# A graph network's start, chunk norms and polynomial: block pattern in three transfers, unit 1 behind unit 0's products, last norm pass on VectorE, first polynomial term a stage ahead

## The chip, the cores and the metric

The kernel runs on one core of one Trainium2 chip. The metric is the device time of one execution in microseconds (us). The executions of one kernel spread over 3 to 10 us, so each kernel was timed several times beside the kernel before on the same chip. Every run of this study was in the fast state, so no state has to be sorted out. Engines: TensorE (PE; its weight loads are PEld), VectorE (DVE), ScalarE (ACT), GpSimd (POOL) and SyncE (SP, which here only issues transfers).

## The reference, cut to what matters

128 graphs of 64 nodes with 256 features pass four layers. Each is `x = layernorm(x + layer(x))`.

```python
# layer 0: five groups of nodes, two graph convolutions each, mixed by softmax(fusion_w)
for g, idx in enumerate(GROUPS):
    h     = relu(norm_adj(adj_g) @ (x_g @ W1[g]) + b1[g])       # 256 -> 512
    out_g = relu(norm_adj(adj_g) @ (h @ W2[g]) + b2[g])         # 512 -> 256
    fused[:, idx] += softmax(fusion_w)[g] * out_g
# layer 1: one symmetric-normalised convolution
# layer 2: polynomial  conv_w[0] + conv_w[1] An + conv_w[2] An^2 + conv_w[3] An^3, applied to x @ W.T, leaky relu
# layer 3: five gated recurrent steps;  m = h @ weight[l];  agg = (adj != 0).T @ m;  h = gru(agg, h)
```

## The kernel before

Layer 0 is done in 16 **units** (some graphs of one group packed into four tiles of up to 126 rows). Layers 1 to 3 work on 16 **chunks** of 8 graphs; the first two chunks' layers 1 and 2 run beside the last units, the rest beside the recurrent steps of earlier chunks. TensorE's order is the program's order. The order of the other engines is found by a scheduler when the kernel is built, from the data dependences and its own estimate of when each thing is ready. This turns out to be the point of the case.

```python
def norm_apply(y, mv, rs, nb, by="v", n=NP, r=128):      # last pass of a layer norm; "a": ACT, "v": DVE
    ...
        if by[p] == "a":
            nc.scalar.activation(v, v, AF.Identity, bias=nb[:r, p : p + 1], scale=rs[:r, p : p + 1])
        else:
            e.tensor_scalar(v, v, mv[:r, p, 0:1], rs[:r, p : p + 1], op0=ALU.subtract, op1=ALU.mult)

def mid(c):                                   # layers 1 and 2 of chunk c, in stages
    a64 = adjs.pop(c)
    Ab = ...; nc.vector.tensor_mul(Ab, a64, pair)          # first to need the chunk's adjacency
    ...                                                    # rsum, rinv, dinv1, dg, An on DVE
    yield
    ...
    nc.scalar.activation(poly, p, AF.Identity, scale=cw[:, 3:4])
    nc.vector.scalar_tensor_tensor(poly, dg, cw[:, 2:3], poly, op0=ALU.mult, op1=ALU.add)
    ...
    norm = norm_stats(xt, "a")                             # twice in a chunk
    yield
    norm_apply(xt, *norm, "a")

def prep(i):                                  # unit i: normalised adjacency A, its transpose AT
    ...
    nc.vector.tensor_add(ae, a, eye0)                      # needs the transfer of a
    ...                                                    # deg, dinv, A = ae * block0
    nc.tensor.transpose(p, A, ident)                       # pT
    evictions.append(nc.vector.tensor_mul(AT, p, dinv))

def aggregate(i): ...                         # pa = xg.T AT  -> ag (ACT copy)
def hidden(i): ...                            # ph = W1 ag    -> hg (ACT relu)
def support(i): ...                           # ps = hg W2    -> s  (ACT copy)
def add(i): ...                               # po = s AT     -> z  (ACT relu, scaled by the softmax)

def others(i): layernorm(XO[i])               # layer 0's norm of the nodes in no group: ten x blocks "xo"
... (cut: other definitions)

block0 = const(c_block0, [TR, 5, TR], "block0", nc.scalar, w0)
...
for i in range(-2, NU + 1):
    if i >= 0: stage(load0, i + 3)
    stage(add, i - 1)
    stage(aggregate, i + 1)
    stage(support, i)
    ...
    if i == -1:
        with tc.issue_after(evictions[0].ins): prep(1)
    else: stage(prep, i + 2)
    if i < 0:
        load0(i + 3, powers[-1]); load_weights(i + 4)
    stage(hidden, i + 1)
    for f, o in ((store_others, i - 1), (others, i), (load_others, i + 2)):
        if 0 <= o < 10: f(o)
    if i == -1: ...                           # softmax of fusion_w: fm, fe (ACT), fs, fr, gw
    elif i == 1: ...                          # late constants on GpSimd's queue; brz = bih + bhh
```

More names in the traces: pp is the product of An with poly (twice in a chunk), h is ACT's copy of the transposed state in a recurrent step, which the product pa of that step (L209) reads, and pf is a product of weights formed once between the two parts. Ab is the first tile of a chunk's polynomial.

Of the kernel before, what the change touches and what calls it, by code (L numbers as in the profile page):

```python
# [9 lines left out]
F32 = mybir.dt.float32  # L10
# [57 lines left out]
def gnn_stack(  # L68
# [58 lines left out]
    def norm_stats(y, by="v", n=NP, r=128):  # L127

        by = (by * n)[:n]
        st = small.tile([128, NP, 6], F32, name="st")  # L130
        mv = small.tile([128, NP, 2], F32, name="mv")
        for p in range(n):
            nc.vector.bn_stats(st[:r, p, :], y[:r, p, :])  # L133
            nc.vector.bn_aggr(mv[:r, p, :], st[:r, p, :])
        ve = small.tile([128, NP], F32, name="ve")
        nc.vector.tensor_scalar(ve[:r, :n], mv[:r, :n, 1], EPS_LN, None, op0=ALU.add)  # L136
        rs = small.tile([128, NP], F32, name="rs")
        nc.gpsimd.tensor_tensor(rs[:r, :n], ve[:r, :n], mhalf[:r, :n], ALU.pow)  # L138
        nb = None
        if "a" in by:  # L140
            nb = small.tile([128, NP], F32, name="nb")
            nc.vector.scalar_tensor_tensor(nb[:r, :n], mv[:r, :n, 0], -1.0, rs[:r, :n], op0=ALU.mult, op1=ALU.mult)  # L142
        return mv, rs, nb

    def norm_apply(y, mv, rs, nb, by="v", n=NP, r=128):
        by = (by * n)[:n]
        for p in range(n):
            v = y[:r, p, :]
# [3 lines that stand above are left out]
                e = nc.vector if by[p] == "v" else nc.gpsimd  # L152
                e.tensor_scalar(v, v, mv[:r, p, 0:1], rs[:r, p : p + 1], op0=ALU.subtract, op1=ALU.mult)
# [64 lines left out]
    def mid(c):  # L218

        a64 = adjs.pop(c)  # L220


        Ab = keep.tile([128, NP, 128], F32, name="Ab", bufs=1)
        nc.vector.tensor_mul(
            Ab.rearrange("p q (b m) -> p q b m", b=2),
            a64[:, :, None, :].to_broadcast([128, NP, 2, N]),
            pair[:, None, :, :].to_broadcast([128, NP, 2, N]),
        )
        A01 = keep.tile([128, NP, 128], F32, name="A01", bufs=4)
        nc.vector.tensor_scalar(A01, Ab, 0.0, None, op0=ALU.not_equal)  # L230
        rsum = small.tile([128, NP], F32, name="rsum")
        nc.vector.tensor_reduce(rsum, a64, AX.X, ALU.add)
        rdeg = small.tile([128, NP], F32, name="rdeg")
        nc.vector.tensor_scalar(rdeg, rsum, 1.0, None, op0=ALU.add)
        rinv = small.tile([128, NP], F32, name="rinv")
        nc.vector.tensor_scalar(rinv, rsum, 1e-9, None, op0=ALU.add)
        nc.vector.reciprocal(rinv, rinv)
        dinv1 = inv_sqrt(rdeg, NP, 128, "d1")

        nc.vector.tensor_scalar(rsum, rsum, 1e-9, None, op0=ALU.add)  # L240
        dg = keep.tile([128, NP, 128], F32, name="dg", bufs=1)
        nc.vector.tensor_mul(
            dg, ident[:, None, :].to_broadcast([128, NP, 128]), rsum[:, :, None].to_broadcast([128, NP, 128])
        )
        An = keep.tile([128, NP, 128], F32, name="An", bufs=1)
        nc.vector.tensor_mul(An, Ab, rinv[:, :, None].to_broadcast([128, NP, 128]))
        yield


        AT1 = keep.tile([128, NP, 128], F32, name="AT1", bufs=1)  # L250
        poly = keep.tile([128, NP, 128], F32, tag="poly", name="poly3", bufs=2)
        p = psum("pT1").rearrange("p (q n) -> p q n", q=NP)
        for q in range(NP):
            nc.tensor.transpose(p[:, q, :], Ab[:, q, :], ident)
        nc.scalar.activation(poly, p, AF.Identity, scale=cw[:, 3:4])

        nc.vector.scalar_tensor_tensor(poly, dg, cw[:, 2:3], poly, op0=ALU.mult, op1=ALU.add)

        nc.vector.tensor_add(AT1, p, ident[:, None, :].to_broadcast([128, NP, 128]))
        nc.vector.tensor_mul(AT1, AT1, dinv1[:, :, None].to_broadcast([128, NP, 128]))  # L260
        yield
        xt = xts.pop(c)
        p = psum("pp").rearrange("p (q n) -> p q n", q=NP)
        for q in range(NP):
            nc.tensor.matmul(p[:, q, :], An[:, q, :], poly[:, q, :], start=True, stop=True)
        poly = keep.tile([128, NP, 128], F32, tag="poly", name="poly1", bufs=2)
        nc.vector.scalar_tensor_tensor(poly, dg, cw[:, 1:2], p, op0=ALU.mult, op1=ALU.add)
        ag = gather(xt, AT1, "ag1")
        nc.vector.tensor_add(xt, xt, l1bs[:, None, :].to_broadcast([128, NP, D]))
        p = psum("pp").rearrange("p (q n) -> p q n", q=NP)  # L270
        for q in range(NP):
            nc.tensor.matmul(p[:, q, :], An[:, q, :], poly[:, q, :], start=True, stop=True)
        poly = keep.tile([128, NP, 128], F32, tag="poly", name="poly0", bufs=2)
        nc.vector.scalar_tensor_tensor(poly, dg, cw[:, 0:1], p, op0=ALU.mult, op1=ALU.add)
        yield
        for u in range(NP // 2):
            p = psum("pd").rearrange("p (q d) -> p q d", q=2)
            for h in range(2):
                q = 2 * u + h
                for k in range(2):  # L280
                    nc.tensor.matmul(  # L281
                        p[:, h, :], ag[:, k, q * 128 : (q + 1) * 128], L1W[:, k, :], start=k == 0, stop=k == 1
                    )
            for h in range(2):
                q = 2 * u + h
                nc.vector.scalar_tensor_tensor(
                    xt[:, q, :], p[:, h, :], dinv1[:, q : q + 1], xt[:, q, :], op0=ALU.mult, op1=ALU.add
                )
        norm = norm_stats(xt, "a")
        yield  # L290
        norm_apply(xt, *norm, "a")
        yield


        ag = gather(xt, poly, "ag2")
        yield
        for u in range(NP // 2):
            p = psum("pd").rearrange("p (q d) -> p q d", q=2)
            for h in range(2):
                q = 2 * u + h  # L300
                for k in range(2):
                    nc.tensor.matmul(  # L302
                        p[:, h, :], ag[:, k, q * 128 : (q + 1) * 128], L2W[:, k, :], start=k == 0, stop=k == 1
                    )
            v = keep.tile([128, 2, D], F32, name="v", bufs=1)
            for h in range(2):
                q = 2 * u + h
                nc.scalar.activation(v[:, h, :], p[:, h, :], AF.Identity, bias=cb, scale=rinv[:, q : q + 1])
            nc.vector.scalar_tensor_tensor(v, v, 0.2, v, op0=ALU.mult, op1=ALU.max)  # L309
            nc.vector.tensor_add(xt[:, 2 * u : 2 * u + 2, :], v, xt[:, 2 * u : 2 * u + 2, :])  # L310
        norm = norm_stats(xt, "a")
        yield
        norm_apply(xt, *norm, "a")
        state[c] = (xt, A01)
        yield

# [11 lines left out]
    with ExitStack() as c0:  # L328
# [187 lines left out]
        eye0 = const(c_eye0, [TR, 5, NJ], "eye0", nc.scalar, w0)  # L516
        load0(0)
        ident = const(c_ident, [128, 128], "ident", nc.scalar)
        block0 = const(c_block0, [TR, 5, TR], "block0", nc.scalar, w0)
        nc.vector.memset(F, 0.0)  # L520
        b1 = const(b1T, [128, NG * 4], "b1", nc.scalar, w0)
        b2c = const(b2.rearrange("g (k p) -> p (g k)", p=128), [128, NG * 2], "b2", nc.scalar, w0)
        fw = spread(fusion_w, NG, "fw", w0, nc.scalar)

        def load_weights(g):
            nc.sync.dma_start(W1[:, g], w1[g].rearrange("(k p) e -> p k e", p=128))
            nc.sync.dma_start(W2[:, g], w2[g].rearrange("(k p) e -> p k e", p=128))

        load_weights(1)

        def products(l, q):

# [22 lines left out]
        for i in range(-2, NU + 1):  # L555
            if i >= 0:
                stage(load0, i + 3)
            stage(add, i - 1)
            stage(aggregate, i + 1)
            early_stage(i, 0)  # L560
            stage(support, i)
            if i == NU:
                folds = [products(0, q) for q in range(3)]
            stage(finish, i - 1, g0)
            early_stage(i, 1)
            if i == -1:

                with tc.issue_after(evictions[0].ins):
                    prep(1)
            else:  # L570
                stage(prep, i + 2)
            if i < 0:
                load0(i + 3, powers[-1])
                load_weights(i + 4)
            stage(hidden, i + 1)
            early_stage(i, 2)
            if i == 0:
                for g in (4, 0):
                    load_weights(g)
            for f, o in ((store_others, i - 1), (others, i), (load_others, i + 2)):  # L580
                if 0 <= o < 10:
                    f(o)
            if i == -1:

                with tc.issue_after(evictions[0].ins):
# [366 lines left out]
```

## Time and profile before

| | before |
|---|---|
| time, median (3 runs; later 6 beside the changed kernel) | 2249.12 us (2248.47) |
| profiled span | 2248.5 us |
| TensorE busy / idle | 2187.8 / 60.7 us |
| ACT / VectorE busy | 1064.2 / 1369.1 us |
| first wait of pp, in the first chunk's polynomial (unit 12's pa is done by then) | 225.44 us |

TensorE is busy 97% of the span, so the reader should look only at who TensorE waits for, and where. The prediction below shows those waits and the places. One place deserves a second look, because its label misled: the 3.38 us at 22.04, which the list of waits puts down to fs. This is VectorE's timeline just before it (start, duration, engine, line, operation, what was written from what; in brackets the idle time before and what ended it):

```profile
20.33 0.43 DVE L133 BATCH_NORM_STATS2 st<-xo 128x6 f32<-128x256 f32 x1 [3.69 <-DMA xo<-in_x_dram]
20.67 0.14 DVE L124 SCALAR_TENSOR_TENSOR d0o<-deg,d0r 126x4 f32<-126x4 f32 x1
...
21.34 0.65 DVE L381 TENSOR_TENSOR A<-ae,block 126x504 f32<-126x504 f32 x1
```

VectorE sat 3.69 us in front of a norm of an x block that had not landed. Behind it in its order stood d0o and A of unit 1, which TensorE needed. A norm that nobody waited for held up the start.

### The profile page before, as it was taken

Reading aid. Unit: us, or ns where it says so; the run is one execution under the profiler, and the core shown is the slowest. Engines: PE = TensorE matmul, PEld = TensorE weight load, DVE = VectorE, ACT = ScalarE, POOL = GpSimd, SP = SyncE. Lnnn points to the kernel's source line nnn. Section 1 sums busy time; section 2 is a strip of 40 time slices with the busy share of each in tenths; the row PEclk is TensorE's granted clock in tenths of the full one; section 3 lists DMA queues with packets and bytes.
Section 4 is the critical chain, followed back from the end, with each engine's and each line's share of the span. In section 5 each row is a group of like instructions: output and inputs, shape, how many; then the busy total and the mean of one; then the engine's idle time right before and its main releaser. Section 6 shows DMA issues by size and latency. Waiting matters only on the chain.

```text
span 2248.5 us, 30146 instructions
## 1 busy us (share of the span) xinstructions
PE 2187.8 (97%) x11526; PEld 1909.7 (85%) x11526; DVE 1369.1 (61%) x2972; ACT 1064.2 (47%) x1978; POOL 603.4 (27%) x639
## 2 busy tenths in 40 slices
PE   6999999999999999999999999999999999999997
PEld 4677788888888888888888888888888888888886
DVE  4543656665766666665756675657665666556546
ACT  2333444445545455445454455455455544455443
POOL 3210123222223223223223232222222232232222
PEclk9999999999999999999999999999999999999998
DMA  6531110000100000000100010001000000000000
GB/s 199 162 118 34 46 43 3 1 3 1 41 1 3 1 20 22 3 1 10 31 1 3 1 40 1 3 1 41 1 1 1 19 10 1 1 10 10 1 1 19
DMA packets 53892, 51.12 MB, mean 23 GB/s; under 512 B 20598, under 2 KB 48630, under 8 KB 53748
## 3 DMA queue, kind: packets, MB, share of 16 engines
q1 hardware_dynamic: 49524, 43.90, 6.4%
q0 software_dynamic: 1936, 4.83, 0.7%
q8 instruction: 91, 1.49, 0.3%
q10 hardware_dynamic: 2288, 0.47, 0.1%
q14 instruction: 53, 0.43, 0.1%
HBM read 32.40 MB, written 16.78 MB: 22 GB/s over the span
## 4 chain that ended last, share of the span: by engine, by line
PE 75%; DVE 13%; ACT 3%; DMA 3%; SPq 2%; issue 2%; POOL 1%; ACTq 0%; POOLq 0%; DVEq 0%
PE parz L688 20%; PE pan L688 10%; PE pdrz L688 10%; PE pa L209 7%; PE pdn L688 5%; PE pbrz L688 5%; PE pT L729 3%; PE ps L430 3%; PE pbn L688 3%; PE pd L281 2%; PE ph L416 2%; DVE st L133 1%; PE pd L302 1%; DMA xo<-in_x_dram 1%; DVE v L309 1%
## 5 line engine op out<-in xcount | busy, mean ns | idle before, releaser
L705 ACT COPY c<-parz 128x512 f32<-128x512 f32 x240 | 140.6, 586 | 343.1 <-PE parz L688 343.0
L688 PE MATMUL parz<-Th,WHH 128*128 128x256 f32 x960 | 285.8, 379 | 0.0
L688 PE MATMUL parz<-Ta,V 128*128 128x256 f32 x960 | 285.6, 379 | 0.0
L668 POOL TENSOR_TENSOR Th<-hn 128x512 f32<-128x512 f32 x64 | 89.3, 1395 | 651.5 <-DVE hn L789 642.1
L786 ACT ACTIVATE NI<-NI,bih 128x512 f32<-128x512 f32 x160 | 115.1, 719 | 191.6 <-DVE NI L782 191.4
L688 PEld LDWEIGHTS parz<-Ta,V 128*128 128x128 f32 x960 | 182.4, 190 | 24.8
L668 POOL TENSOR_TENSOR Ta<-agg 128x512 f32<-128x512 f32 x80 | 101.6, 1270 | 377.9 <-ACT agg L212 377.9
L705 ACT COPY c<-pan 128x512 f32<-128x512 f32 x240 | 140.8, 587 | 127.4 <-PE pan L688 127.4
L688 PEld LDWEIGHTS parz<-Th,WHH 128*128 128x128 f32 x960 | 176.2, 190 | 20.8 <-ACT c L705 0.2
L717 DVE TENSOR_TENSOR RZ<-pdrz,c 128x512 f32<-128x512 f32 x80 | 55.1, 689 | 200.7 <-PE pdrz L688 200.6
L759 ACT ACTIVATE RZ<-RZ,brz 128x512 f32<-128x512 f32 x160 | 106.7, 715 | 117.0 <-DVE RZ L717 117.0
L688 PE MATMUL pan<-Ta,V 128*128 128x256 f32 x480 | 143.1, 380 | 0.9 <-ACT c L705 0.9
L688 PE MATMUL pan<-Th,WHH 128*128 128x256 f32 x480 | 142.8, 379 | 0.0
L711 DVE TENSOR_TENSOR NI<-pbn,c 128x512 f32<-128x512 f32 x80 | 55.3, 691 | 137.5 <-PE pbn L688 135.1
L209 PEld LDWEIGHTS pa<-A,h 128*128 128x128 f32 x1024 | 123.2, 192 | 17.8 <-ACT h L803 15.2
L209 PE MATMUL pa<-A,h 128*128 128x128 f32 x1024 | 126.1, 276 | 9.6 <-ACT h L803 9.6
L138 POOL TENSOR_TENSOR rs<-ve,mhalf 128x4 f32<-128x4 f32 (+2 forms) x66 | 67.7, 1026 | 248.3 <-DVE ve L136 248.3
L707 DVE TENSOR_TENSOR NI<-pdn,c 128x512 f32<-128x512 f32 x80 | 55.2, 690 | 118.8 <-ACT c L705 118.8
L150 ACT ACTIVATE xt<-xt,nb,rs 128x256 f32<-128x256 f32 x186 | 99.6, 595 | 52.0 <-DVE nb L142 51.8
L787 DVE TENSOR_TENSOR RZ<-hn,NI 128x512 f32<-128x512 f32 x128 | 87.9, 687 | 53.0 <-ACT NI L786 53.0
L789 DVE TENSOR_TENSOR hn<-RZ,NI 128x512 f32<-128x512 f32 x160 | 109.6, 685 | 1.8
L788 DVE TENSOR_TENSOR RZ<-RZ 128x512 f32<-128x512 f32 x160 | 109.5, 684 | 1.8
(199 smaller groups left out, 5147.1 us busy)
## 6 DMA issues: line engine op xcount, KB each, us to landing
out_dram<-xt SPq DMA_DIRECT2D x32, 256.0 KB
W<-in_w_dram SPq DMA_DIRECT2D x10, 512.0 KB
xt<-xb SPq DMA_DIRECT2D x32, 156.0 KB
xo<-in_x_dram SPq DMA_DIRECT2D x9, 512.0 KB
xb<-xo SPq DMA_DIRECT2D x9, 512.0 KB
xt<-xa SPq DMA_DIRECT2D x32, 100.0 KB
xg<-in_x_dram SPq DMA_DIRECT2D x25, 125.0 KB
xa<-xg SPq DMA_DIRECT2D x25, 125.0 KB
```

The source lines that it names most:

```text
L138: nc.gpsimd.tensor_tensor(rs[:r, :n], ve[:r, :n], mhalf[:r, :n], ALU.pow)
L150: nc.scalar.activation(v, v, AF.Identity, bias=nb[:r, p : p + 1], scale=rs[:r, p : p + 1])
L209: nc.tensor.matmul(p[:, q * 128 : (q + 1) * 128], src[:, q, k * 128 : (k + 1) * 128], m[:, q, :], start=True, stop=True)
L430: nc.tensor.matmul(p[: u.rows[t], t - v, :], hg[:, e, u.off[t] : u.off[t] + u.rows[t]], W2[:, u.g, e, :], start=e == 0, stop=e == 3,)
L668: nc.gpsimd.tensor_sub(t[:, 0:2, :], a[:, :, H:], a[:, 0, :].rearrange("p (s n) -> p s n", s=2))
L688: nc.tensor.matmul(bank[:, g, :], w[:, q, i - 1, :], rhs, start=i in (1, 2, 5) and g == 0 and m == 0, stop=m == len(side) - 1, skip_group_ ...
L705: nc.scalar.copy(c, self.a)
L759: nc.scalar.activation(RZ[:, q, 0, :], RZ[:, q, 0, :], AF.Sigmoid, bias=b[0])
L786: nc.scalar.activation(n, n, AF.Tanh, bias=bih[:, 4 + j : 5 + j])
L787: nc.vector.tensor_sub(d, self.hT[:, j, :], n)
L788: nc.vector.tensor_mul(d, d, z)
L789: nc.vector.tensor_add(self.hn[:, j, :], d, n)
```

## The change

The intent: let TensorE begin sooner (only the block's first part must land; unit 0's products no longer stand behind unit 1's transposes; the weights' loads are split so that data come in the order of need), take the chunk norms' last pass off ACT, where they stood ahead of copies that TensorE waits for, and form the polynomial's second-degree term while the transposes still run. The ten x norms move one unit later.

```diff
@@ mid
+        poly = keep.tile([128, NP, 128], F32, tag="poly", name="poly3", bufs=2)
+        nc.scalar.activation(poly, dg, AF.Identity, scale=cw[:, 2:3])
         An = keep.tile([128, NP, 128], F32, name="An", bufs=1)
 ... (cut: next stage)
-        nc.scalar.activation(poly, p, AF.Identity, scale=cw[:, 3:4])
-        nc.vector.scalar_tensor_tensor(poly, dg, cw[:, 2:3], poly, op0=ALU.mult, op1=ALU.add)
+        nc.vector.scalar_tensor_tensor(poly, p, cw[:, 3:4], poly, op0=ALU.mult, op1=ALU.add)
 ... (cut; the next four lines twice)
-        norm = norm_stats(xt, "a")
+        norm = norm_stats(xt)
         yield
-        norm_apply(xt, *norm, "a")
+        norm_apply(xt, *norm)
@@ start
-        block0 = const(c_block0, [TR, 5, TR], "block0", nc.scalar, w0)
+        block0 = w0.tile([TR, 5, TR], F32, name="block0")
+        for ks in (slice(1, 2), slice(2, 5), slice(0, 1)):
+            nc.scalar.dma_start(block0[:, ks], c_block0[:, ks])
 ... (cut: load_weights becomes load_first for W1 and load_second for W2)
-            stage(aggregate, i + 1)
+            if i:
+                stage(aggregate, i + 1)
             stage(support, i)
+            if not i:
+                aggregate(1)
             if i == -1:
+                hidden(0)
                 with tc.issue_after(evictions[0].ins):
                     prep(1)
             else:
                 stage(prep, i + 2)
-            if i < 0:
-                load0(i + 3, powers[-1])
-                load_weights(i + 4)
-            stage(hidden, i + 1)
+                stage(hidden, i + 1)
+            if i == -2:
+                load0(1, powers[0]); load_second(1); load0(2, powers[0]); load_first(2)
+            elif i == -1:
+                load_second(2); load_first(3)
+            elif i == 0:
+                load_second(3)                      # then both of groups 4 and 0
 ... (cut: the old place of the loads of groups 4 and 0)
-            for f, o in ((store_others, i - 1), (others, i), (load_others, i + 2)):
-                if 0 <= o < 10:
-                    f(o)
+            for f, j in ((store_others, i - 1), (others, i), (load_others, i + 2)):
+                for o in range(10):
+                    if min(o + 1, 9) == j:
+                        f(o)
```

More of the change, by code (lines that the diff above doesn't have):

```diff
@@ L250, in mid @@
         AT1 = keep.tile([128, NP, 128], F32, name="AT1", bufs=1)
-        poly = keep.tile([128, NP, 128], F32, tag="poly", name="poly3", bufs=2)
         p = psum("pT1").rearrange("p (q n) -> p q n", q=NP)
@@ L310, in mid @@
             nc.vector.tensor_add(xt[:, 2 * u : 2 * u + 2, :], v, xt[:, 2 * u : 2 * u + 2, :])
-        norm = norm_stats(xt, "a")
+        norm = norm_stats(xt)
         yield
-        norm_apply(xt, *norm, "a")
+        norm_apply(xt, *norm)
         state[c] = (xt, A01)
@@ L523, in gnn_stack, with load_first, load_second @@
         fw = spread(fusion_w, NG, "fw", w0, nc.scalar)
-        def load_weights(g):
+        def load_first(g):
             nc.sync.dma_start(W1[:, g], w1[g].rearrange("(k p) e -> p k e", p=128))
+        def load_second(g):
             nc.sync.dma_start(W2[:, g], w2[g].rearrange("(k p) e -> p k e", p=128))
-        load_weights(1)
+        load_first(1)
         def products(l, q):
@@ L571, in gnn_stack @@
                 stage(prep, i + 2)
-            if i < 0:
-                load0(i + 3, powers[-1])
-                load_weights(i + 4)
-            stage(hidden, i + 1)
-            early_stage(i, 2)
-            if i == 0:
-                for g in (4, 0):
-                    load_weights(g)
-            for f, o in ((store_others, i - 1), (others, i), (load_others, i + 2)):
-                if 0 <= o < 10:
-                    f(o)
+                stage(hidden, i + 1)
+            if i == -2:
+                load0(1, powers[0])
+                load_second(1)
+                load0(2, powers[0])
+                load_first(2)
+            elif i == -1:
+                load_second(2)
+                load_first(3)
+            elif i == 0:
+                load_second(3)
+                for g in (4, 0):
+                    load_first(g)
+                    load_second(g)
+            early_stage(i, 2)
+            for f, j in ((store_others, i - 1), (others, i), (load_others, i + 2)):
+                for o in range(10):
+                    if min(o + 1, 9) == j:
+                        f(o)
             if i == -1:
```

## The prediction

> **What bounds the kernel now.** I read the page's busy shares first, to see which engine sets the end, then who TensorE waited for, then the timeline around each of those waits, then the groups by shape for the cost of what moves.
>
> ```profile
> span 2248.5 us, 30146 instructions
> PE 2187.8 (97%) x11526; PEld 1909.7 (85%) x11526; DVE 1369.1 (61%) x2972; ACT 1064.2 (47%) x1978; POOL 603.4 (27%) x639
> ```
>
> TensorE is occupied for all but 2248.5 - 2187.8 = 60.7 us. The change adds and removes no matmul, so it can gain only what lies in those 60.7 us, plus what a slow matmul clock costs after a gap. The view of TensorE's waits (releaser: total us, times, longest) says where they lie:
>
> ```profile
> PE pT L389 <- DVE A L381: 13.0, 1, 13.0
> PE pa L209 <- ACT h L803: 9.6, 14, 0.7
> PE pp L272 <- DVE poly L267: 7.2, 7, 1.3
> PE pT L729 <- DVE hn L789: 5.4, 2, 4.1
> PE pT L389 <- DVE fs L591: 3.4, 1, 3.4
> PE pa L402 <- DVE AT L392: 3.3, 2, 2.5
> PE po L452 <- ACT s L439: 3.0, 1, 3.0
> PE pp L272 <- DVE d1z L118: 2.7, 5, 0.5
> ```
>
> The 5.4 us on hn are in the last 50 us, which the change does not touch. The rest falls into four places, the first being the start (timeline; start, duration, engine, line, what; in brackets the idle time before and its releaser):
>
> ```profile
> 12.27 0.68 DVE L381 TENSOR_TENSOR A<-ae,block 126x504 f32<-126x504 f32 x1 [4.45 <-DMA block<-in_c_block_dram]
> ...
> 15.40 1.28 ACT L589 ACT_TABLE_LOAD   x1 [15.40 <-DMA fw<-in_fusion_w_dram]
> ...
> 17.00 0.58 ACT L406 COPY ag<-pa 128x504 f32<-128x504 f32 x1
> ...
> 22.04 1.04 PE L389 MATMUL pT<-ident,A 126*126 126x126 f32 x4 [3.38 <-DVE fs L591]
> 22.87 8.28 PE L416 MATMUL ph<-ag,W 128*128 128x504 f32 x16
> ...
> 111.89 1.98 PE L402 MATMUL pa<-AT,xg 126*128 126x126 f32 x12 [2.52 <-DVE AT L392]
> ```
>
> VectorE waits 4.45 us for the block pattern before TensorE has anything to do. Later unit 1's transposes, blocked on VectorE, stand ahead of unit 0's hidden products (ph), whose last input was ready at 19.28 (the second ag copy, 18.70 + 0.58). At 111.89 a layer norm of the x loads stands before AT in VectorE's order. The last two places are ACT's (chunk norms xt L150):
>
> ```profile
> 439.54 0.60 ACT L150 ACTIVATE xt<-xt,nb,rs 128x256 f32<-128x256 f32 x1 [1.46 <-DVE nb L142]
> ...
> 440.40 0.57 ACT L803 COPY h<-pT 128x512 f32<-128x512 f32 x1
> ...
> 441.02 2.05 PE L209 MATMUL pa<-A,h 128*128 128x128 f32 x16 [0.69 <-ACT h L803]
> ```
>
> ACT sat 1.46 us in order behind nb, ran one norm pass, then half a gate, and only then the h copy that TensorE needed. The 3.0 us wait on s at 314.96 is the same thing: four norm passes from 312.58 to 314.65 stand before the s copies.
>
> **What the Trainium skill says.** "VectorE: DVE Perf Modes", section "The perf-mode tier table": fp32 tensor_scalar in SBUF runs at 2x, tensor_tensor at 1x, and any PSUM operand drops a tier. The trace agrees in kind: 128x512 takes 426 ns as tensor_scalar (A01 L230) and about 685 as tensor_tensor. The moved norm pass is a tensor_scalar in SBUF, so its existing VectorE form can be used for its price. "TensorE: Matmul & The Clock Gate", section "What's actually happening": the clock is halved by default and released after about 3.4 us of activity. The trace agrees: four transposes take 1.10 us at 13.01 and 0.60 later; the first ph takes 8.28 us against 7.03 for the next of that shape; after the 2.52 us gap at 111.89 the ps group takes 8.86 instead of 7.07, at a granted clock of 0.73 in 115 to 120. So a gap of a few us can cost up to 1.8 us more. "DMA: Bandwidth & Descriptors", section "Queues, rings and completion order": each DMA engine round-robins between queues by packet. The trace shows the block's queue sharing the engines with the weights' queue from 7 to 11 us.
>
> **The change, part by part.**
>
> *Norms.* The page's rows by shape give the prices:
>
> ```profile
> L150 ACT ACTIVATE xt<-xt,nb,rs 128x256 f32<-128x256 f32 x186 | 99.6, 595 | 52.0 <-DVE nb L142 51.8
> L142 DVE SCALAR_TENSOR_TENSOR nb<-mv,rs 128x4 f32<-128x4 f32 x47 | 7.7, 163 | 50.2 <-POOL rs L138 50.2
> L153 DVE TENSOR_SCALAR xo<-xo,mv,rs 128x256 f32<-128x256 f32 x39 | 13.7, 409 | 11.2 <-POOL rs L138 11.2
> ```
>
> 16 chunks x 2 norms x 4 = 128 of the 186 passes leave ACT (58 stay): 128 x 0.595 = 76 us. VectorE gets 128 x 0.409 = 52 and loses 32 nb x 0.163 = 5, so it goes from 61% to about 63%. None of this is bound; what counts is order. In the order of the built programs the pattern "c, c, h, RZ, xt, RZ, h, RZ" on ACT stands 14 times before and not once after. I take off the whole **9.6 us**. The s copy now directly follows the z activations, so the 3.0 us at 314.96 go too, with about 1.3 us of slow clock behind it (24 pf in 6.85 us there, 5.35 later): **4.3 us**.
>
> *Polynomial.* Same counts: one ACT pass of 0.69 us (now from SBUF) and one VectorE pass of about 0.78. The first pp never waits in the profile; the waits of 7.2 + 2.7 us are of the second pp, for poly L267, which is not touched and has the same seven instructions before it in VectorE's order after the change. **0 us.**
>
> *Start.* The block goes in thirds by kind; kind 1, the first needed, is 63.5 of 310 KB. Its data should move right behind ident's, which left about 7.5 us, so landing (some 2 us behind its data, as before) near 9.5: A about 2.8 us earlier. But ACT's order still has the softmax of the fusion weights (table load, fe) before the first ag copy, and those wait for fw, which landed at 15.40. In the built program the transfers of both hardware queues share eight completion counters in turn, and two more transfers now stand ahead; b1 now waits for unit 0's W1, and fw stands behind it. I take fw at 15.4 to 16.5, so ag at 17 to 18 and, with the second copy, ph at 18.2 to 19.5 instead of 22.87: about 4 us, not the 4.45 + 3.38 that the waits suggest.
>
> *What is left at 115 us.* From 46 to 125 us the SP queue issues back to back (0.74 us each with 0.04 between, some 16 a unit). Its head loses one W or x load of 512 KB in front of unit 3, so I put it 3.5 to 4.5 us earlier. But VectorE's new order puts AT(2) behind brz (whose bhh landed at 47.5), AT(3) and AT(4) behind a whole norm of x, and AT(5) behind unit 7's adjacency. From the old times less these shifts, TensorE should meet waits of 0 to 3 us at units 2 to 5, and no longer the 2.52 at unit 6. Net at 115 us, with the slow clock there: **4.5 us**, the softest term.
>
> Sum: 9.6 + 4.3 + 0 + 4.5 = 18.4; 2249.1 - 18.4 = 2230.7.
>
> **Rivals.** (1) *fw or brz takes the block's place*: TensorE's start waits for whatever is last; the listed waits speak for it. Then the start gives 0 to 1 us: about 2235. (2) *All the start is kept*: against it, SP issues without a pause; a start 7 us earlier plus the clock would make 2226. (3) *VectorE becomes late*: 1.4 us of norm now stand before gate work (RZ<-pdrz) and could delay TensorE. For it: in-order VectorE at 63%, with the pp waits already there. Against it: matmuls of the gates show no wait on VectorE at all in 350 to 2200 us, and hn has several us until its transpose. If each of 28 norms cost 0.5 us: 14 us back, about 2245. (4) *ACT was only the last of several*: h copies might still be late from sigmoids; then half of 9.6 stays, about 2236.
>
> **Range and chances.** The norm term is firm (14 like waits, one cause), the start is worth 0 to 8, VectorE's delay 0 to 10 the other way. 2231, with 2222 to 2241 for eight in ten. Two per cent is 45 us; all idle time is 60.7, so faster by that much is next to excluded, and slower would need new waits of 45 us.
>
> **What would show it.** Right: ACT busy near 989, VectorE near 1415; "pa <- ACT h" gone from TensorE's waits; no wait for s near 312; A at 9 to 10 us; ph starting at 18 to 20, with fw or fe before ag; pp waits still about 10 us; idle time of TensorE about 43 us. Wrong: ph before 17 or after 21, a wait of over 3 us for AT at units 2 to 7, or gate matmuls waiting for VectorE.

## The result, and the profile after

The changed kernel took 2236.01 us (median of 6 fast runs, 2234.59 to 2241.92) against 2248.47 us for the kernel before in the same rounds (2246.98 to 2251.53). The ratio is 0.9949, with a 95% interval of 0.9936 to 0.9962: within 2%, about 11.5 us faster. A ratio here is the mean time of one kernel's fast runs over the mean of the other's of the same rounds, so it is not quite the ratio of the medians.

The page's span and busy shares of the kernel after:

```profile
span 2234.4 us, 30150 instructions
PE 2184.9 (98%) x11526; PEld 1912.4 (86%) x11526; DVE 1402.4 (63%) x3068; ACT 1003.4 (45%) x1850; POOL 596.4 (27%) x639
```

TensorE's idle time fell from 60.7 to 2234.4 - 2184.9 = 49.5 us; the prediction had 43. Next, TensorE's waits (releaser: total us, times, longest), to be held against the list in the prediction:

```profile
PE pT L389 <- DVE A L381: 9.5, 1, 9.5
PE pp L272 <- DVE rinv L236: 8.5, 10, 1.5
PE pa L402 <- DVE AT L392: 7.4, 4, 2.9
...
PE pa L402 <- DMA a<-in_adj_dram: 1.7, 1, 1.7
PE pp L272 <- ACT NI L802: 1.4, 1, 1.4
PE ph L416 <- ACT ag L406: 1.3, 1, 1.3
```

The fourteen waits of pa on h (9.6 us), the one of po on s (3.0) and the one put down to fs (3.4) are gone. The waits of pp only changed their names. But pa's waits on AT rose from 3.3 to 7.4 us, with 1.7 us on a transfer beside them. TensorE's timeline shows where:

```profile
9.47 1.10 PE L389 MATMUL pT<-ident,A 126*126 126x126 f32 x4 [9.47 <-DVE A L381]
...
16.43 8.70 PE L416 MATMUL ph<-ag,W 128*128 128x504 f32 x16 [1.31 <-ACT ag L406]
...
57.64 2.04 PE L402 MATMUL pa<-AT,xg 112*128 112x112 f32 x16 [1.68 <-DMA a<-in_adj_dram]
...
72.39 2.04 PE L402 MATMUL pa<-AT,xg 112*128 112x112 f32 x16 [1.31 <-DVE AT L392]
...
91.99 3.43 PE L402 MATMUL pa<-AT,xg 126*128 126x126 f32 x16 [2.43 <-DVE AT L392]
...
128.88 3.66 PE L402 MATMUL pa<-AT,xg 126*128 126x126 f32 x16 [2.88 <-DVE AT L392]
```

Unit 0's products (ph) begin 22.87 - 16.43 = 6.44 us sooner than before. Then units 3, 4, 5 and 7 wait, 8.3 us in all as shown, and two of the gaps also slow the clock: the same pa group takes 3.43 and 3.66 us where it took 1.96 and 2.05, and the granted clock is 0.50 from 91.5 to 94.9 and from 129.1 to 132.4 us. At unit 7 nothing of the gain is left, although the kernel before has its own wait of 2.52 us at unit 6.

One caution: the 6.44 us are of one pair of traces. In seven other profiled runs with the new start (e3, e5, e7, e9, e10, e13, e15 below) ph of unit 0 begins at 17.58 to 18.24 us, and in e1 and e6, which have the old one, at 21.86 and 21.63. Some 4 us is the usual gain at this point.

TensorE's order being fixed, the starts of the same group of matmuls in two traces can be subtracted. This table gives the start of pa of each unit (us), from the profiled runs of four kernels; the last two are experiments that follow:

| | ph 0 | pa 2 | pa 3 | pa 5 | pa 6 | pa 7 | pa 8 |
|---|---|---|---|---|---|---|---|
| before | 22.87 | 48.64 | 61.17 | 91.45 | 111.89 | 128.46 | 144.92 |
| after | 16.43 | 43.17 | 57.64 | 91.99 | 111.22 | 128.88 | 146.91 |
| e9_at_then_chunks | 17.58 | 44.03 | 56.56 | 86.84 | 104.60 | 119.22 | 135.53 |
| e12_old_start_at_first | 19.55 | 43.97 | 56.50 | 86.78 | 104.54 | 119.15 | 141.42 |

After against before: 6.4 us ahead at ph 0, level at unit 7, 2.0 us behind at unit 8. The same subtraction later on gives the other terms: 2.0 us behind at the first wait of pp (225.44 against 227.43), 1.0 ahead at 390 us, so 3.0 gained around the s copies; then fourteen steps of 0.85 us, one for each wait on h that went (11.9 us), each followed by one of 0.10 (pa itself takes 1.95 us and no longer 2.05; 1.4 us in all). The steps at pp, the polynomial's, sum to -0.3 us. It is 14.0 ahead at the last of these groups, 14.1 in the span.

Why AT is late is seen in VectorE's timeline of the kernel after, ahead of unit 5's AT:

```profile
88.91 0.26 DVE L370 TENSOR_TENSOR ae<-a,eye 126x12 f32<-126x12 f32 x2 [4.39 <-DMA a<-in_adj_dram]
...
91.26 0.68 DVE L392 TENSOR_TENSOR AT<-pT,d0o 126x504 f32<-126x504 f32 x1
```

The additions at 88.91 are those of unit 7. VectorE idled 4.39 us for their transfer, and AT of unit 5, whose transposes had long been done (81.18 us), stood behind them. AT of units 3 and 4 came directly behind a norm of an x block, AT of unit 7 behind two. Unit 3's wait is AT's too, whatever its label: AT ended at 57.59 us, pa began at 57.64.

### The profile page after: what moved, and what is told of

Its sections match the earlier page's. It is cut to its first block, busy times and chain, and to the rows that moved or that the text cites. A ratio compares the mean times of both kernels' runs of the same rounds, so it can differ in the third digit from the quotient of the medians.

```text
span 2234.4 us, 30150 instructions
## 1 busy us (share of the span) xinstructions
PE 2184.9 (98%) x11526; PEld 1912.4 (86%) x11526; DVE 1402.4 (63%) x3068; ACT 1003.4 (45%) x1850; POOL 596.4 (27%) x639
## 4 chain that ended last, share of the span: by engine, by line
PE 86%; DVE 7%; DMA 2%; issue 2%; POOL 1%; SPq 1%; ACT 0%; ACTq 0%; POOLq 0%; DVEq 0%
PE parz L704 23%; PE pdrz L704 12%; PE pan L704 12%; PE pa L209 8%; PE pdn L704 6%; PE pbrz L704 6%; PE pT L745 4%; PE pbn L704 3%; PE ph L416 3%; PE ps L430 3%; PE pd L281 2%; PE pd L302 2%; DMA xo<-in_x_dram 1%; PE pp L272 1%; PE pa L402 1%
## 5 line engine op out<-in xcount | busy, mean ns | idle before, releaser
L797 DVE SCALAR_TENSOR_TENSOR NI<-NI,bhh,RZ 128x256 f32<-128x256 f32 (+1 forms) x160 | 105.1, 657 | 2.0
```

The lines of the kernel that those rows point to most:

```text
L797: nc.vector.scalar_tensor_tensor(n[:, j, f], h, bhh[:, 4 + j : 5 + j], r[:, j, f], op0=ALU.add, op1=ALU.mult)
```

## The experiments

**Theory A**: VectorE's program order spends the start's gain; AT and A stand behind work whose data land late. **Rival B**: SyncE issues one transfer each 0.75 us, so the data come no sooner, whatever the order. **Rival N**: the norms carry everything and the start is worth nothing in any order. Beside these, the parts were run alone. All kernels gave correct results; each is compared with the kernel before on its own chip (medians of the latter 2248.58, 2248.02 and 2247.69 us in the three batches).

| run | median us | runs | ratio to before | 95% |
|---|---|---|---|---|
| e1_norms_only | 2232.03 | 5 | 0.9925 | 0.9913 to 0.9937 |
| e2_start_only | 2256.55 | 6 | 1.0035 | 1.0022 to 1.0047 |
| e7_at_first | 2239.59 | 5 | 0.9956 | 0.9944 to 0.9968 |
| e5_xg_pool | 2238.69 | 5 | 0.9960 | 0.9947 to 0.9972 |
| e9_at_then_chunks | 2226.23 | 4 | 0.9897 | 0.9882 to 0.9912 |
| e10_both | 2229.28 | 6 | 0.9910 | 0.9896 to 0.9923 |
| e6_poly_only | 2252.64 | 14 | 1.0010 | 1.0000 to 1.0020 |
| e3_old_others | 2235.17 | 6 | 0.9935 | 0.9923 to 0.9947 |
| e15_best_again | 2226.19 | 4 | 0.9909 | 0.9896 to 0.9923 |
| e12_old_start_at_first | 2226.25 | 5 | 0.9910 | 0.9896 to 0.9925 |
| e13_best_no_poly | 2228.03 | 5 | 0.9911 | 0.9898 to 0.9923 |
| e14_softmax_later | 2229.36 | 5 | 0.9915 | 0.9901 to 0.9928 |

### The parts alone

**e1_norms_only**: the kernel before with only this:

```diff
-        norm = norm_stats(xt, "a")           # both norms of a chunk
+        norm = norm_stats(xt)
-        norm_apply(xt, *norm, "a")
+        norm_apply(xt, *norm)
```

> The kernel before with nothing changed but the last pass of the chunk norms on VectorE (start, x blocks and polynomial as before). Theory N (the norms alone carry more than the whole gain, and the start gives nothing): 2231 to 2235 us, 14 to 17 under the kernel before; the fourteen waits of pa on ACT's h copies and the 3.0 us wait of po on the s copies are gone, and the start is that of the kernel before (ph of unit 0 near 22.9 us, pa of unit 7 near 128.5). Rival S (start and polynomial each carry a part, as the prediction had it, 4.5 us of the start): 2236 to 2240 us, since the norms alone would then be worth only 7 to 11.

Measured 2232.03 us: the norms alone are worth some 17 us, more than the whole change. The waits on h and s were gone, as theory N had it. In the trace the fourteen steps of 0.85 us are there again, and 3.6 us between 225 and 390 us. A part is luck of the build: the 2.52 us wait before unit 6 also vanished (pa 6 at 108.45), though nothing of that stage was edited. The scheduler had found another order. At the first pp wait this trace is 4.2 us ahead of the kernel before, where the changed kernel is 2.0 behind.

**e2_start_only**: the changed kernel with norms and polynomial put back.

> The changed kernel with the norms and the polynomial as they were: only the start (block in three, unit 1 behind unit 0's products, split weight loads, x norms one unit later). Theory N: the 6.4 us that unit 0 gains are all spent by unit 7, so the time is 2247 to 2251 us, within 2 us of the kernel before; ph of unit 0 near 16.4 us but pa of unit 7 at 128 to 129 and behind a halved clock. Rival S (the start's gain survives to 115 us): 2242 to 2245 us, 4 to 6 under the kernel before. Both: the waits of pa on h stay 14, near 9.6 us.

Measured 2256.55 us, some 8 us *slower* than before: neither number held. The direction is theory N's, and stronger. TensorE's waits in its trace:

```profile
PE pa L209 <- ACT h L819: 10.0, 14, 1.0
...
PE pa L402 <- DVE AT L392: 6.8, 4, 3.4
```

The AT waits are of the same kind as in the changed kernel, here at units 3, 4 and 7. ph of unit 0 came at 19.75 us, behind a wait of 3.7 us on ag, and pa 7 at 131.38 us. In the profiled run the loss against before was 4.5 us at the first pp wait (229.98 against 225.44) and 5.3 in the span; the rest of the 8 us is not in that one trace.

**e6_poly_only**: the kernel before with the polynomial's part of the diff alone.

> The kernel before with the polynomial's first term formed a stage ahead and nothing else changed. The prediction's step (the wait of pp only changes its name): 2246 to 2251 us, within 2 us of the kernel before; the waits of pp before their products together still 9 to 12 us, on rinv or NI instead of poly and d1z. Rival (the earlier first term takes the wait away): waits of pp under 4 us and 2241 to 2244 us.

Measured 2252.64 us, ratio 1.0010: nothing, or 2 us lost. The waits of pp are 8.5 us on rinv, 1.4 on NI and 0.2 on poly, 10.1 together against 9.9: the step of the prediction. The median is above the expected 2251, by less than the runs scatter (2247.3 to 2254.9).

The three parts taken alone add up to -17 + 8 + 2 = -7 us, the whole gives -11.5. They need not add: each build gets its own order on VectorE. At the first pp wait e1 was 4.2 us and e6 3.2 us ahead of the kernel before, with nothing of that stage edited, and e2 4.5 behind. So e6 alone does not price the polynomial; e13 below does it better.

### Order or transfers?

**e7_at_first**: the changed kernel; three edits to the order, no instruction more or less.

```diff
         def others(i):
-            layernorm(XO[i], n=XO[i].shape[1])
+            with tc.issue_after(evictions[-1].ins):          # behind the newest AT
+                layernorm(XO[i], n=XO[i].shape[1])
@@ prep
-                    nc.vector.tensor_add(ae..., a..., eye0...)
+                    with tc.issue_after(evictions[-1].ins) if evictions else nullcontext():
+                        nc.vector.tensor_add(ae..., a..., eye0...)
@@ brz is formed at i == 4 instead of i == 1
```

> The changed kernel with VectorE's program order alone changed: in each unit of the start the eviction AT stands ahead of that iteration's x norm and of the next unit's adjacency, and brz is formed later. No instruction is added or removed. Theory A (the start's gain is lost because AT stands behind x norms and adjacency additions whose data land late): waits of pa on AT fall from 7.4 us to under 2, pa of unit 7 comes at 122 to 125 us instead of 128.9, and the time is 2229 to 2232 us. Theory B (SyncE issues a transfer every 0.75 us and the a and x tiles land no earlier than the changed kernel uses them, so order does not matter): the waits turn to waits on the transfers of a or xg or on A, pa of unit 7 stays at 127 to 129 us, and the time is 2234 to 2237 us.

The time, 2239.59 us, missed theory A's number by 8 us. It lies above rival B's 2234 to 2237 too, but by the time alone B would have been believed. The trace says otherwise: waits on AT fell to 0.8 us, and pa 6 came at 105.40 us, 5.8 us ahead of the changed kernel. Then a new wait took everything back. VectorE's timeline, and TensorE's:

```profile
119.46 0.69 DVE L224 TENSOR_TENSOR Ab<-a,pair 128x512 f32<-128x512 f32 x1 [17.62 <-DMA a<-in_adj_dram]
```

```profile
121.70 1.10 PE L390 MATMUL pT<-ident,A 126*126 126x126 f32 x4 [7.30 <-DVE A L382]
```

The first instruction for chunk 0 (Ab) had been put ahead of A of unit 7, although TensorE transposes Ab only at 213.81 us. VectorE idled 17.62 us for the chunk's adjacency while unit 7's own data were there. The wait had moved along VectorE's queue.

**e5_xg_pool**: the changed kernel with the x tiles of units 3 to 8 on GpSimd's queue, so that SyncE issues half as many.

```diff
-            qx = nc.gpsimd if i < 3 else nc.sync
+            qx = nc.gpsimd if i < 9 else nc.sync
```

> The changed kernel with the x tiles of units 3 to 8 fetched by GpSimd's queue instead of SyncE's: SyncE has half as many transfers to issue in the start, so adjacency tiles and x blocks land earlier. VectorE's order shifts somewhat with it. Theory B (SyncE's issue rate holds the start): the wait of pa on the adjacency transfer and the AT waits fall to under 3 us together, pa of unit 7 at 122 to 126 us, 2229 to 2232 us. Theory A (the order on VectorE holds it): AT waits stay at 5 us or more because AT still stands behind x norms, 2233 to 2237 us. A third outcome is that GpSimd's issues delay its powers or x tiles, so that waits of pa on xg or of dinv appear, and the time is over 2237.

Measured 2238.69 us, 1.7 us over what theory A expected. The AT waits stayed (7.1 us, the longest 4.39 before unit 3, where AT stood directly behind a norm of x again). The faster issue gave nothing. It is no clean test of B, for GpSimd's issues did delay it, somewhat as in the third outcome: before unit 2 a norm waited 2.85 us for its rs, which stood behind the x transfers in GpSimd's order, and AT behind it cost TensorE 1.92 us.

**e9_at_then_chunks**: e7 with one more edge, from AT of unit 7 to the whole first stage of a chunk.

```diff
@@ mid, first stage
+        with tc.issue_after(evictions[9].ins):               # AT of unit 7
             Ab = ...                                         # and all up to the first yield
```

> As the run with AT ahead of the x norms, and the first stage of the recurrent chunks' polynomial (Ab and what follows it on VectorE) may not stand ahead of AT of unit 7 any more. In the earlier run that stage, waiting for the adjacency of a chunk, held VectorE for 17.6 us at 101.8 to 119.5 us and PE waited 7.3 us for A of unit 7. Theory A (VectorE's order alone spends the start's gain): pa of unit 7 comes at 121 to 124 us (before 128.5, changed kernel 128.9), no wait of PE on VectorE between 30 and 200 us is over 1 us, and the time is 2227 to 2231 us, 5 to 9 under the changed kernel. Theory B (the transfers of the later units come too late for it anyway): a wait on A or on a transfer appears at unit 6, 7 or 8, pa of unit 7 at 127 or later, 2234 us or more.

Measured 2226.23 us, 10 us under the changed kernel's median, 0.8 under theory A's range, and 23 us (1%) under the kernel before by the ratio. TensorE's waits at the start are down to the first one, which these edits do not touch, and small ones (0.8 us on AT, 1.5 of ph on ag):

```profile
PE pT L391 <- DVE A L383: 10.4, 1, 10.4
PE pp L273 <- DVE rinv L237: 8.5, 10, 1.5
...
PE pa L404 <- DVE AT L394: 0.8, 1, 0.8
```

pa 7 came at 119.22 us, sooner than theory A had asked. Rival B falls, the issue rate being the same: the data of units 2 to 8 were there in time.

**e10_both**: e9 with the edit of e5.

> As the run before it in this list, with the x tiles of units 3 to 8 on GpSimd's queue too. Theory A: VectorE's order was the whole loss, so this gives nothing more: within 2 us of that run. Theory B (SyncE's 0.75 us per issued transfer holds the start): 3 us or more under that run. If GpSimd's own issues delay its powers, a wait on dinv or A of over 2 us appears and it is slower.

2229.28 us; no gain over e9. It is 3 us more by the medians where theory A had said within 2, but their intervals overlap. In the trace A of unit 4 was 1.33 us late. Rival B had wanted 3 us less.

**e3_old_others**: the changed kernel with the x norms at their old places (the last hunk of the diff undone).

> The changed kernel with the x norms (and their loads and stores) back one unit earlier, where the kernel before has them. Theory A (AT loses behind x norms whose blocks land late, and it makes it no better that the norm comes a unit earlier, for its block is then later still against it): AT waits of 7 us or more, 2235 to 2241 us. Rival X (moving the x norms a unit later is what spends the start's gain): AT waits under 4 us, pa of unit 7 at 122 to 125 us, 2229 to 2232 us.

2235.17 us, the changed kernel's time. AT waits 5.5 us, between the two expectations, with 2.92 us before unit 3 and 1.77 before unit 7. So it is not the moved x norms as such; in either place some AT ends up behind one.

### What is the start worth in a good order?

**e15_best_again** is e9 unchanged, on the chip of the next three. **e12_old_start_at_first** is the kernel before with the norms on VectorE and the order edges of e9: old block transfer, old order on TensorE, old weight loads, old polynomial. **e13_best_no_poly** is e9 with the polynomial undone. **e14_softmax_later** is e9 with the softmax of the fusion weights one step later (at i == 0, behind AT of unit 1).

> The kernel of the run with AT ahead of the x norms and of the chunks, once more and on the chip of the next three, which each differ from it in one part. 2224 to 2229 us; pa of unit 7 at 119 to 122 us.

> The kernel before with the norms on VectorE and the same order on VectorE (AT ahead of the x norms, brz later, the chunks' stage behind AT of unit 7), but with the old start and the old polynomial. Theory A (the start's gain is real and was only spent in VectorE's order): ph of unit 0 near 22 us, pa of unit 7 at 122.5 to 124.5 us, 2230 to 2233 us, that is 4 to 6 us over the run with the new start. Rival (the order is worth it alone and the new start is worth nothing even then): within 2 us of the run with the new start.

> As the best kernel with the polynomial undone. The prediction's step (nothing either way): within 1.5 us of the best kernel, waits of pp on poly and d1z (about 10 us) in place of those on rinv and NI. Rival P (the polynomial costs what the run of it alone seemed to show, 1 to 4 us): 1.5 us or more under the best kernel.

> As the best kernel, with the softmax of the fusion weights behind unit 0's copies and AT of unit 1, so that ACT's first ag copies no longer stand behind the transfer of fw. Theory F (fw takes the block pattern's place in front of ph): the wait of ph of unit 0 on ag (1.5 us) goes, ph of unit 0 comes about 1.5 us sooner, and the time is 1 to 2 us under the best kernel. Rival: the wait moves to the next thing that lands late (W1 or unit 1's A), and the time is within 0.7 us.

All four are level: 0.9909 to 0.9915 with some 0.0013 to either side, or 3 us. So neither theory F's gain of 1 to 2 us (e14) nor rival P's cost of the polynomial (e13) is seen; from 390 us to the last matmuls, the stretch with most chunks' polynomials, e13's trace gains 13.3 us on the kernel before and e15's 13.1. For e12 this contradicts what I expected of theory A and is its rival's answer, and rival N's: **with VectorE's order mended, the old start is as good as the new one**, to within 3 us. Its trace shows why. Without the norm of x ahead of unit 1's A, the old start's second wait falls from 3.38 to 0.26 us:

```profile
19.06 0.65 PE L391 MATMUL pT<-ident,A 126*126 126x126 f32 x4 [0.26 <-DVE A L383]
```

From unit 2 to unit 7 the two starts are within 0.1 us of each other in the table above, although block lands later in the old one (VectorE waited 4.17 us for it) and ph 0 comes 2 us later than in e9. Two things take the 2 us away. In e9 ph of unit 0 stands behind its wait of 1.48 us on ag (the softmax) and takes 8.52 us; in e12 it takes 6.93, for its first matmuls are no longer slow. And e12 has then done unit 1's transposes, which still take e9 0.4 us. In e14, with no wait there, ph takes 7.01 us and pa 2 comes at 40.41, against 43.97 in e12.

At unit 8 e12's profiled run lost ground, and so did e14's. Both happened to be the slowest of their five runs (2232.40 and 2231.09 us), so the two traces may show more of this than the other runs had. VectorE and TensorE in e12:

```profile
125.09 0.69 DVE L225 TENSOR_TENSOR Ab<-a,pair 128x512 f32<-128x512 f32 x1 [8.40 <-DMA a<-in_adj_dram]
```

```profile
130.58 0.54 PE L391 MATMUL pT<-ident,A 126*126 126x126 f32 x3 [4.20 <-DVE A L383]
```

It is the same Ab, now one unit later: still ahead of unit 8's A, and in these runs the chunk's adjacency was issued by SyncE at 121.0 us (116.9 in e14), against 110.95 in e15. e14 shows it at its clearest. Its softmax edit did what theory F said and more: ph of unit 0 began at 15.47 us instead of 18.24 and pa 7 at 117.12 instead of 119.78. Then unit 8 waited 5.09 us behind Ab.

Left open: whether the new start or the later softmax would pay if Ab stood behind unit 8 as well. The runs of this study were used up.

One comparison puts the gain in its place. The norms alone (e1) are at 0.9925. The start, the polynomial and all order edges together add only some 4 us to that in e15 (0.9909) and 6 in e9 (0.9897); e1's interval overlaps e15's. At the first wait of pp the changed kernel is 2.0 us behind the kernel before, e1 4.2 ahead and e9 9.4 ahead: half of what the edges win against the changed kernel only restores what another build (e1) had without them.

## Why the prediction was right or wrong

It gave 2231 us and a range of 2222 to 2241; 2236.01 lies inside, 5 us over its centre. By its own steps:

- **Norms, 9.6 us: right in mechanism, too small.** No wait on h is left, and each was worth 0.85 us, not 0.69, and 0.10 more in the pa behind it: 13.3 us. The idle time in the trace counts from the end that the profile models for the matmul before. Gate matmuls in pairs start 0.43 us apart but are shown with 0.59, so every shown wait leaves out 0.16 us. e1 has the same fourteen steps.
- **The s copies, 4.3 us: right, but not all of it stayed.** The wait is gone, and with the clock behind it the next products end 4.9 us sooner. The stretch from 225 to 390 us gave only 3.0 us (3.6 in e1): a wait of pp on mv grew from 0.51 to 1.23 us, and one on w (2.17 us at 329.02) came before a stretch at half clock (0.50 from 330.5 to 333.8).
- **Polynomial, 0 us: right.** pp's waits are 10.1 us against 9.9, the steps at pp sum to -0.3 us; e6 and e13 show no gain.
- **Start up to ph: right in kind, put a little too late.** A was formed from 8.73 us on, predicted for 9 to 10. ph began at 16.43, under the 17 that the text itself named as a sign of error: fw landed at 14.3, not 15.4 to 16.5. It still stood behind the softmax. The scored trace was an early one: in the seven other runs named above ph came at 17.6 to 18.2 us, so the term of about 4 us up to ph holds. The other sign, a wait of over 3 us for AT, missed narrowly (2.88).
- **"Net at 115 us, with the slow clock there: 4.5 us, the softest term": this step failed.** It was -2.0 us at the first pp wait. The prediction had seen which AT stand behind what, and four of its five places were right: waits at units 3, 4 and 5, none at 6. At unit 2 brz did stand ahead of AT, but bhh landed at 42.7 us and not 47.5, just in time. It did not see unit 7 (2.88 us, behind two norms of x), and it gives no sum from which its 4.5 us follow. Waits of 1.7, 1.3, 2.4 and 2.9 us and 3.1 us of slow clock in two pa groups (3.43 - 1.96 and 3.66 - 2.05) exceed the 6.4 us gained; the 2.52 us saved at unit 6, with some 1.8 us of slow clock, went the same way. What the runs put in its place: the start is worth what VectorE's order lets through. With AT ahead of late work it keeps its lead to unit 7 (e9), and then the old start does the same (e12).
- **Rivals.** None of the four was the outcome. Rival 1 has the nearest time (2235) and was right that fw would stand before ph (a wait of 1.31 us), but not that the start would gain nothing there. Rival 3 (VectorE late) looked for the harm among the gates, where no wait on VectorE appeared; VectorE was late in the start, from its order and not from the passes added to it: e2, without them, waits on AT as well (6.8 us). VectorE's busy time of 1402 us (1415 predicted) shows again that the share says nothing about it.
- **Busy times.** ACT came to 1003 us, not 989. The page's rows of the norm passes after:

```profile
L153 DVE TENSOR_SCALAR xt<-xt,mv,rs 128x256 f32<-128x256 f32 x130 | 47.2, 408 | 32.8 <-POOL rs L138 32.8
...
L150 ACT ACTIVATE xt<-xt,nb,rs 128x256 f32<-128x256 f32 x58 | 30.1, 589 | 8.1 <-DVE nb L142 7.9
```

ACT's passes fell from 99.6 to 30.1 us of busy time, 69.5 and not 76: passes in a row overlap, so 128 times the mean of one was too much, on both engines. The engine's total fell by 60.8 only. No other row of ACT rose by 9 us (the polynomial's pass, the most, from 11.0 to 11.5), so part of what the passes occupied was shared with their neighbours.

In the profiled pair 18.4 us were forecast and 14.1 came: the gates gave 3.5 us more (13.1 with the polynomial's -0.3), the s copies 1.3 less, the start 6.5 less. That the time was only 5 us off is in part luck: an error in the gates made up half of the one in the start. The range left 10 us upwards, enough even for the start's error alone.

## What to carry to other kernels

Where a scheduler sets the order of an in-order engine, list what stands ahead of each result that the bounding engine needs, and ask for each when its data land; an early start buys nothing past the first such place. Give late-landing, unhurried work an explicit edge behind the urgent results, and keep adding edges until the wait has left the queue: one edge (e7) only moved it, the next (e9) came out 10 us under the changed kernel. Judge a part of a change in the context of a good order, since a build of one part alone also gets a new order: in e1 and e6 that alone took away the wait before unit 6.

## What the Trainium skill lacked or had wrong

- "Perfetto Trace Analysis", section "Tensor Engine Instruction (MATMUL, LD_WEIGHTS)", says that the end of a TensorE instruction is a model and not a measurement. It lacks the consequence: shown waits are too short, here 0.69 us where the next start came 0.85 us late. The same note calls VectorE strict FIFO. The runs agree and put a price on it that the page lacks: one instruction waiting 17.62 us for a transfer held A of unit 7 and cost TensorE 7.30 us.
- "TensorE: Matmul & The Clock Gate", section "What's actually happening", gives an idle window of about 3.4 us before the clock drops. Here gaps shown as 1.88 (e2), 2.43 and 2.88 us already slowed the pa group behind them (3.76, 3.43 and 3.66 us instead of 2.04, 1.96 and 2.05), while after one of 1.77 us (e3) it took 2.05. The slow stretch need not begin with that group: after a gap of 1.92 us that ended at 46.71 (e5) the granted clock was 1.00 to 48.9 and 0.50 from 49.0 to 52.3. The page calls the window free-running; no run here tests how much of one a gap must fill.
- "SBUF — State Buffer", section "SBUF: two separate sides", says that a VectorE instruction with two SBUF inputs and a GpSimd one that reads SBUF exclude each other. The durations fit that the change moved such a collision rather than removing it, though no run tests it: with one input in PSUM the polynomial pass fell from 951 to 748 ns on average, and the pass after the next (AT of a chunk) rose from 878 to 1285 ns, also in e6. The page lacks a hint that freeing one instruction exposes the next. VectorE and GpSimd before, then after:

```profile
466.56 1.06 POOL L669 TENSOR_TENSOR Ta<-agg,Ta 128x256 f32<-128x256 f32 x1
...
466.96 1.22 DVE L257 SCALAR_TENSOR_TENSOR poly<-dg,cw,poly 128x512 f32<-128x512 f32 x1
```

```profile
465.45 1.23 POOL L686 TENSOR_TENSOR Ta<-agg,Ta 128x256 f32<-128x256 f32 x1
...
466.01 1.21 DVE L260 TENSOR_TENSOR AT<-AT,d1o 128x512 f32<-128x512 f32 x1
```
